# A gated recurrence on one core: another order for the products of half B, and for three VectorE operations

## The chip, the core and the metric

The kernel runs on one core of one Trainium2 chip. The metric is device time in microseconds for one execution. Times of one kernel are given as the median of several executions; the profile is of one execution, taken by the hardware profiler.

## What is computed

A recurrent layer over 512 steps with a batch of 8 and 512 units, plus a residual. Cut to what matters:

```python
def step(h, x_t):
    fused = sigmoid(concatenate([x_t, h], -1) @ w_W + w_b)
    r, z = split(fused, 2, axis=-1)          # hidden_state, output_state
    memory = x_t @ wx_W + wx_b + r * (h @ wh_W + wh_b)
    h_new = z * h + (1 - z) * tanh(memory)
    return h_new, h_new
_, hs = scan(step, h0, xT)                   # 512 steps
return x + swapaxes(hs, 0, 1)
```

Everything is in float32. What is written below as hh is `h @ wh_W + wh_b`. A step needs the whole h of the step before, so the steps follow one another strictly.

## The kernel before

**How the work is tiled.** The 512 units lie as four blocks of 128: block k holds, on 128 partitions, the units with which product k is made. Half A is the two blocks 0 and 1, half B the blocks 2 and 3. The state of each half lies transposed in SBUF (hTA and hTB), so that it can be the stationary operand of a matmul; a ring of eight buffers for each half holds the states of eight steps, four steps side by side in one buffer ("slots", GS = 4). A product `A2`, say, is one block k = 2 of the state against the weight columns of bank A, as four matmuls, one for each group of 32 columns of the array (line 136 issues all of them). In the trace every such matmul stands as two passes, so that one product is 8 records.

**What goes where.** There are three PSUM banks for the products of a step, each in two copies that alternate every four steps (`WH`, line 25): bank A (192 columns) takes hh, z and r of half A; bank Z (64 columns) takes z of half B; bank B (128 columns) takes r and hh of half B. Each bank has to have its products with all four blocks before it can be read. Blocks 0 and 1 need hTA of the step before, blocks 2 and 3 need hTB.

**TensorE's order** is written out by hand, in line 23, and run in lines 212 to 217 for each step: the names of bank and block in turn, and at the end one of four parts of the input product for a later group of four steps (`xp`, 384 columns, `prefill`). With the order before, the first three products need hTA alone (A0, B0, A1), then A2 and A3 (hTB), so that bank A is complete after five products; then the rest of B; then the four of Z.

**The elementwise part of a step** is in the functions of lines 229 to 290, and the order in which they are called (lines 292 to 303) is the order of VectorE's queue; the schedule is set by hand (`manual_schedule`), so nothing is moved. For half hf (0 is A, 1 is B):

- `turn_r`: VectorE transposes the r columns out of PSUM (tr, line 231), then ScalarE's sigmoid writes md0 (line 150).
- `turn_h`: VectorE transposes hh out of PSUM into md1 (md in the trace, line 243).
- `turn_z`: VectorE transposes z (tz, line 231), then ScalarE makes z (zA or zB) and 1 - z (hd0).
- `memory`: VectorE forms r * hh + x part with one scan instruction (m, line 263), then ScalarE's tanh writes hd1.
- `kept`: VectorE multiplies z and the old state (line 274), also into hd1; it waits for ScalarE's z.
- `update`: VectorE forms the new state with a second scan (hTA or hTB, line 283); it waits for tanh and for `kept`.

After these follow one transpose of the input part (line 179), on some steps a ScalarE copy that seeds the next banks (lines 157 and 174), and GpSimd's residual addition (line 314). SP issues the loads of x and the stores of the output, one of each in 16 steps.

The core of the order before is:

```python
        turn_r(0)
        turn_h(0)
        turn_z(0)
        memory(0)
        turn_h(1)
        kept(0)
        turn_r(1)
        update(0)
        turn_z(1)
        memory(1)
        kept(1)
        update(1)
```

Of the kernel before, what the change touches and what calls it, by code (L numbers as in the profile page):

```python
# [19 lines left out]
DVE_FILL = 5  # L20
SYNC = mybir.DependencyInfo(mybir.DependencyClass.Sync, mybir.DependencyReason.DATA)

ORDER = "A0 B0 A1 A2 A3 B1 B2 B3 Z0 Z1 Z2 Z3"

WH = {"A": slice(0, 192), "Z": slice(192, 256), "B": slice(256, 384)}

# [4 lines left out]
def tile_cond_rnn_residual(  # L31
# [44 lines left out]
    def load_x(c):  # L76
        if c < NCH:
            t_ = xin_p.tile([P, NQ, TC * B], F32, tag="xin", name=f"xin_{c}")
            nc.sync.dma_start(out=t_, in_=x[c].rearrange("p (k n) -> p k n", k=NQ))  # L79
            xins[c] = t_  # L80
# [36 lines left out]
    def state(hf, i):  # L117

        s = i % GS
        return hT[hf][i % NH][:, B * s : B * s + B, :, 1]  # L120
# [14 lines left out]
    def mm(out_, lhsT, rhs, start=False):  # L135
        nc.tensor.matmul(  # L136
            out_, lhsT, rhs, start=start, stop=False, skip_group_check=True
        )
# [10 lines left out]
    def act(key, *args, **kw):  # L149
        inst = nc.scalar.activation(*args, **kw).ins  # L150
        if key in written:
            tc.declare_no_dep(inst, written[key], reason="ordered through VectorE")
        written[key] = inst

    def seed(g):

        nc.scalar.copy(xps[g % 2], bias)

    def prefill(g):

        c, t0 = divmod(g * GS, TC)
        for k in range(NQ):
            for j in range(NQ):
                mm(
                    xps[g % 2][32 * j : 32 * j + 32, 64:448],
                    xins[c][:, k, t0 * B : t0 * B + 32],
                    wx[:, k, j, :],
                )
            yield

    def spread(g, names):

        for n in names:
            nc.scalar.copy(banks[g % 2][n], xps[g % 2][:, XP[n]])

    def turn_x(g, e):

        c0 = XP["X"].start + 32 * e
        nc.vector.transpose(
            md1[g % 2][:, e // 2, :, e % 2, 1], xps[g % 2][:, c0 : c0 + 32]  # L180
        )

    def take(it, n=None):
        while n is None or n > 0:
            if next(it, it) is it:
                return
            n = None if n is None else n - 1
# [14 lines left out]
    for i in range(T):  # L202
        g, s = divmod(i, GS)
        c, t = divmod(i, TC)
        ps = banks[g % 2]
        if t == 0:
            load_x(c + 3)
            ot = out_p.tile([P, NQ, TC, B], F32, tag="ot", name=f"ot_{c}")
        if s == 0:
            pre = prefill(g + 2) if g + 2 < NG else iter(())  # L210

        for n in ORDER.split():
            bank, k = n[0], int(n[1])
            hs = hT[k // 2][i % NH][:, :, k % 2, 1]
            for j in range(NQ):
                mm(ps[bank][32 * j : 32 * j + 32, :], hs, wh[:, k, j, WH[bank]])
        take(pre, 1)

        rows = slice(B * s, B * s + B)
        def flat(t_):  # L220
            return t_.rearrange("p n c s -> p (n c s)")

        raw = {
            "h": (ps["A"][:, :HU], ps["B"][:, HU:]),
            "z": (ps["A"][:, HU : 2 * HU], ps["Z"]),
            "r": (ps["A"][:, 2 * HU :], ps["B"][:, :HU]),
        }

        def turned(n, hf):
            t_ = work.tile([P, 2, 32], F32, tag=f"t{n}{hf}", name=f"t{n}{hf}_{i}")  # L230
            nc.vector.transpose(t_.rearrange("p c n -> p (c n)"), raw[n][hf])  # L231
            return t_[:, :, rows]

        def turn_r(hf):
            act(
                ("r", hf, g % 2, s),
                md0[hf][g % 2][:, rows, :, 1].rearrange("p n c -> p c n"),
                turned("r", hf),
                AF.Sigmoid,
            )  # L240

        def turn_h(hf):
            inst = nc.vector.transpose(  # L243
                md1[g % 2][:, hf, :, :, 0].rearrange("p n c -> p c n"), raw["h"][hf]
            ).ins

            if hf == 0 and i + 1 - NH in pool_done:
                tc.add_manual_dep(inst, pool_done[i + 1 - NH].name, SYNC)

        def turn_z(hf):  # L250
            tz = turned("z", hf)
            act(("z", hf, i % 2), zs[hf][i % 2], tz, AF.Sigmoid)
            act(
                ("zc", hf, i % 2),
                hd0[hf][i % 2][:, :, :, 1].rearrange("p n c -> p c n"),
                tz,
                AF.Sigmoid,
                scale=-1.0,
            )

        def memory(hf):
            m = work.tile([P, B, 2, 2], F32, tag=f"m{hf}", name=f"m{hf}_{i}")
            nc.vector.tensor_tensor_scan(  # L263
                flat(m),
                flat(md0[hf][g % 2][:, rows]),
                flat(md1[g % 2][:, hf, rows]),
                0.0,
                ALU.mult,
                ALU.add,
            )  # L270
            act(("n", hf, i % 2), hd1[hf][i % 2][:, :, :, 0], m[:, :, :, 1], AF.Tanh)

        def kept(hf):
            nc.vector.tensor_tensor(
                hd1[hf][i % 2][:, :, :, 1],
                zs[hf][i % 2].rearrange("p c n -> p n c"),
                state(hf, i),
                ALU.mult,
            )

        def update(hf):
            s1 = (i + 1) % GS
            nc.vector.tensor_tensor_scan(  # L283
                flat(hT[hf][(i + 1) % NH][:, B * s1 : B * s1 + B]),
                flat(hd0[hf][i % 2]),
                flat(hd1[hf][i % 2]),
                0.0,
                ALU.mult,
                ALU.add,
            )  # L290

        turn_r(0)
        turn_h(0)
        turn_z(0)
        memory(0)
        turn_h(1)
        kept(0)
        turn_r(1)
        update(0)
        turn_z(1)  # L300
# [4 lines that stand above are left out]
        if g + 1 < NG:  # L305
            turn_x(g + 1, s)
            if s == 0:
                spread(g + 1, "A")
            elif s == 1:
                spread(g + 1, "BZ")  # L310
            elif s == 3 and g + 3 < NG:
                seed(g + 3)
        for hf in range(2):
            pool_done[i + 1] = nc.gpsimd.tensor_tensor(  # L314
                ot[:, 2 * hf : 2 * hf + 2, t, :].rearrange("p c n -> p n c"),
                xins[c][:, 2 * hf : 2 * hf + 2, t * B : t * B + B].rearrange("p c n -> p n c"),
                state(hf, i + 1),
                ALU.add,
            ).ins
        if t == TC - 1:  # L320
            nc.sync.dma_start(out=out[c], in_=ot.rearrange("p k t b -> p (k t b)"))
            xins.pop(c)
# [62 lines left out]
```

## Time and profile before

| what | value |
|---|---|
| median of 3 executions | 1726.7 us (1726.22 to 1728.58) |
| the profiled execution's own time | 1726.31 us |
| span of the profiled execution | 1724.5 us |
| TensorE matmuls busy | 1706.2 us, 99% of the span |
| TensorE weight loads busy | 1489.8 us, 86% |
| VectorE busy | 1138.6 us, 66% |
| ScalarE busy | 894.8 us, 52% |
| GpSimd busy | 252.9 us, 15% |
| granted TensorE clock | 0.997 |

How to read it: a name such as `A<-wh,hTA` is the output and the inputs of an instruction. PE is TensorE's matmuls, PEld its weight loads, DVE is VectorE, ACT ScalarE, POOL GpSimd. The busy time of matmuls counts overlapping records once and their ends are modelled, so that 99% doesn't say by itself that TensorE works at its full rate; the distances between starts say more. A wait is put down to the instruction that came last. Times inside a step are given from the start of the first matmul of A0, in ns, where they are medians over the steps of the trace.

### The profile page before, as it was taken

The page shows a single profiled execution, that of the slowest core. Times are in us where ns is not written, and L with a number is a line of the kernel's source. Part 1 is how long each engine was busy: PE and PEld are TensorE (multiplying, and loading weights), DVE is VectorE, ACT ScalarE, POOL GpSimd, SP SyncE. Part 2 cuts the span into 40 slices and gives each one's busy share as a digit, 9 for nine tenths or more (in the row PEclk, how much of TensorE's full clock was granted, in tenths as well). Part 3 has the DMA queues.
Part 4 walks back from the last instruction along what each step waited for, and adds up shares of the span by engine and source line. Part 5 has one row for each costly group of instructions (what it writes and reads, how often), then busy time and mean ns, then how long its engine had stood idle before and what let it go on. Part 6 is the DMA issues. An engine that isn't in the chain of part 4 may idle for free.

```text
span 1724.5 us, 121032 instructions
## 1 busy us (share of the span) xinstructions
PE 1706.2 (99%) x53312; PEld 1489.8 (86%) x53312; DVE 1138.6 (66%) x6663; ACT 894.8 (52%) x4610; POOL 252.9 (15%) x1048
## 2 busy tenths in 40 slices
PE   7999999999999999999999999999999999999998
PEld 5888888888888888888888888888888888888887
DVE  2666666666666666666666666666666666666666
ACT  3555555555555555555555555555555555555554
POOL 1111111111111111111111111111111111111111
PEclk9999999999999999999999999999999999999999
DMA  4000000000000000000000000000000000000000
GB/s 179 17 4 17 17 17 17 10 11 17 17 17 16 5 17 17 17 16 5 17 17 17 17 17 5 17 17 17 17 4 17 16 17 16 5 17 11 11 11 10
DMA packets 11232, 31.09 MB, mean 18 GB/s; under 512 B 1360, under 2 KB 1360, under 8 KB 10704
## 3 DMA queue, kind: packets, MB, share of 16 engines
q1 hardware_dynamic: 10704, 23.35, 3.9%
q8 instruction: 416, 6.82, 1.6%
q14 instruction: 112, 0.92, 0.2%
HBM read 14.96 MB, written 8.39 MB: 14 GB/s over the span
## 4 chain that ended last, share of the span: by engine, by line
PE 98%; DMA 1%; DVE 0%; issue 0%; SPq 0%; ACT 0%; POOLq 0%; POOL 0%; DVEq 0%
PE A L136 39%; PE B L136 25%; PE xp L136 19%; PE Z L136 14%; DMA hin<-in_h_dram 1%; DMA wx<-in_wx_dram 0%; DVE tr L231 0%; ACT md0A L150 0%; DVE hTA L283 0%; DVE m L263 0%; SPq L85 0%; DVE md L243 0%; SPq L79 0%; POOLq L379 0%; POOL ot L314 0%
## 5 line engine op out<-in xcount | busy, mean ns | idle before, releaser
L136 PE MATMUL A<-wh,hTA 128*32 128x192 f32 x8192 | 555.6, 327 | 9.5 <-DVE hTB L125 7.3
L136 PEld LDWEIGHTS A<-wh,hTA 128*32 128x32 f32 x8192 | 321.3, 137 | 184.6 <-DVE hTA L283 176.2
L136 PE MATMUL B<-wh,hTA 128*32 128x128 f32 x8192 | 450.9, 273 | 0.0
L136 PE MATMUL A<-wh,hTB 128*32 128x192 f32 x8192 | 448.3, 327 | 0.0
L136 PE MATMUL xp<-wx,xin 128*32 128x384 f32 x4096 | 444.2, 486 | 0.0
L231 DVE STREAM_TRANSPOSE tr<-A 128x64 f32<-128x64 f32 x512 | 128.0, 250 | 470.0 <-PE A L136 470.0
L150 ACT ACTIVATE md0A<-tr 128x16 f32<-128x16 f32 x512 | 121.1, 236 | 487.9 <-DVE tr L231 487.9
L136 PEld LDWEIGHTS B<-wh,hTA 128*32 128x32 f32 x8192 | 364.7, 136 | 1.6
L136 PE MATMUL B<-wh,hTB 128*32 128x128 f32 x8192 | 336.4, 273 | 0.0
L136 PEld LDWEIGHTS A<-wh,hTB 128*32 128x32 f32 x8192 | 302.4, 137 | 33.0 <-DVE hTB L283 1.2
L314 POOL TENSOR_TENSOR ot<-xin,hTA 128x16 f32<-128x16 f32 x512 | 125.5, 245 | 1119.5 <-DVE hTA L283 1031.6
L136 PEld LDWEIGHTS B<-wh,hTB 128*32 128x32 f32 x8192 | 266.6, 137 | 0.0
L136 PE MATMUL Z<-wh,hTB 128*32 128x64 f32 x8192 | 240.6, 226 | 0.0
L136 PE MATMUL Z<-wh,hTA 128*32 128x64 f32 x8192 | 235.0, 223 | 0.0
L136 PEld LDWEIGHTS Z<-wh,hTA 128*32 128x32 f32 x8192 | 218.5, 141 | 0.0
L136 PEld LDWEIGHTS Z<-wh,hTB 128*32 128x32 f32 x8192 | 200.1, 148 | 0.0
L314 POOL TENSOR_TENSOR ot<-xin,hTB 128x16 f32<-128x16 f32 x512 | 124.5, 243 | 348.5 <-DVE hTB L283 343.2
L150 ACT ACTIVATE md0B<-tr 128x16 f32<-128x16 f32 x512 | 119.2, 233 | 70.8 <-DVE tr L231 0.7
L283 DVE TENSOR_TENSOR_SCAN hTB<-hd0B,hd1B 128x32 f32<-128x32 f32 x512 | 115.2, 225 | 52.7
L263 DVE TENSOR_TENSOR_SCAN m<-md0B,md 128x32 f32<-128x32 f32 x512 | 147.6, 288 | 0.0
L243 DVE STREAM_TRANSPOSE md<-B 128x64 f32<-128x64 f32 x512 | 146.9, 287 | 0.0
L243 DVE STREAM_TRANSPOSE md<-A 128x64 f32<-128x64 f32 x512 | 139.0, 271 | 0.0
(43 smaller groups left out, 1835.8 us busy)
## 6 DMA issues: line engine op xcount, KB each, us to landing
xin<-in_x_dram SPq DMA_DIRECT2D x32, 256.0 KB, 2.9
out_dram<-ot SPq DMA_DIRECT2D x32, 256.0 KB, 2.1
wx<-in_wx_dram SPq DMA_DIRECT2D x4, 768.0 KB, 6.7
wh<-in_wh_dram SPq DMA_DIRECT2D x4, 768.0 KB, 13.5
bias<-in_bias_dram SPq DMA_DIRECT2D x4, 64.0 KB, 2.0
hin<-in_h_dram SPq DMA_DIRECT2D x1, 16.0 KB, 14.8
```

The source lines that it names most:

```text
L136: nc.tensor.matmul(out_, lhsT, rhs, start=start, stop=False, skip_group_check=True)
L150: inst = nc.scalar.activation(*args, **kw).ins
L231: nc.vector.transpose(t_.rearrange("p c n -> p (c n)"), raw[n][hf])
L243: inst = nc.vector.transpose(md1[g % 2][:, hf, :, :, 0].rearrange("p n c -> p c n"), raw["h"][hf]).ins
L263: nc.vector.tensor_tensor_scan(flat(m), flat(md0[hf][g % 2][:, rows]), flat(md1[g % 2][:, hf, rows]), 0.0, ALU.mult, ALU.add,)
L283: nc.vector.tensor_tensor_scan(flat(hT[hf][(i + 1) % NH][:, B * s1 : B * s1 + B]), flat(hd0[hf][i % 2]), flat(hd1[hf][i % 2]), 0.0, ALU.mu ...
L314: pool_done[i + 1] = nc.gpsimd.tensor_tensor(ot[:, 2 * hf : 2 * hf + 2, t, :].rearrange("p c n -> p n c"), xins[c][:, 2 * hf : 2 * hf + 2, ...
```

## The change

Two lines of order are changed, and nothing else:

```diff
-ORDER = "A0 B0 A1 A2 A3 B1 B2 B3 Z0 Z1 Z2 Z3"
+ORDER = "A0 B0 A1 A2 A3 B1 Z0 B2 Z1 B3 Z2 Z3"
...
         turn_h(0)
         turn_z(0)
         memory(0)
+        kept(0)
         turn_h(1)
-        kept(0)
         turn_r(1)
         update(0)
         turn_z(1)
```

On TensorE the products Z0 and Z1, which need hTA alone, move in between the products of bank B, so that B3 is followed by Z2 and Z3. On VectorE `kept` of half A (z * h) moves from behind the transpose of hh of half B to in front of it; behind it now stand the transposes of hh and r of half B, and then the update of half A. The instructions are the same in number and shape, and the queues of ScalarE, GpSimd and SP hold the same order.

## The prediction

> **What bounds the kernel now.** I read the page first for the chain that ended last, then that chain in order of time over one step, then who waits for whom, then VectorE's own timeline over the same step. The chain lies on TensorE almost wholly:
>
> ```profile
> PE 98%; DMA 1%; DVE 0%; issue 0%; SPq 0%; ACT 0%; POOLq 0%; POOL 0%; DVEq 0%
> ```
>
> The chain in order of time, one step of the recurrence (columns: start, length, what):
>
> ```profile
> 1004.10 0.33 PE A L136 x8
> 1004.43 0.22 PE B L136 x8
> 1004.65 0.97 PE A L136 x24
> 1005.62 0.64 PE B L136 x24
> 1006.26 0.48 PE Z L136 x29
> 1006.74 0.67 PE xp L136 x8
> 1007.41 0.25 PE A L136 x5
> ```
>
> A step lasts 1007.41 - 1004.10 = 3.31 us without a hole. Times 512 steps that is 1695 of the span's 1724.5; the rest is the lead-in and the tail. Each product of the code stands here as two passes over four column groups, 8 records. A product into A costs 0.97/3 = 0.32, into B 0.64/3 = 0.21, into Z 0.48/4 = 0.12, and the input product xp 0.67. By columns (192, 128, 64, 384) that is 1.7 ns each, but Z takes 1.9: the narrow products alone do not stream at the others' rate. Within the Z run, the starts of successive passes in this trace are 55, 57, 57, 63, 61, 63, 62 and 63 ns apart: the first two or three after a wide product go at 55 to 57[...].
>
> The waits say what is nearly as long as TensorE's own work:
>
> ```profile
> PEld A L136 <- DVE hTA L283: 176.2, 506, 0.5
> ...
> PEld A L136 <- DVE hTB L283: 1.2, 7, 0.2
> ```
>
> The weight load of A0 waits for hTA in nearly every step, behind the cover of xp. The load of A2 waits for hTB too, but its wait is hidden behind A1's stream. VectorE over the same step (start, length, operation):
>
> ```profile
> 1002.35 0.25 DVE L231 STREAM_TRANSPOSE tr<-A 128x64 f32<-128x64 f32 x1 [0.92 <-PE A L136]
> 1002.52 0.27 DVE L243 STREAM_TRANSPOSE md<-A 128x64 f32<-128x64 f32 x1
> 1002.65 0.21 DVE L231 STREAM_TRANSPOSE tz<-A 128x64 f32<-128x64 f32 x1
> 1002.90 0.23 DVE L263 TENSOR_TENSOR_SCAN m<-md0A,md 128x32 f32<-128x32 f32 x1
> 1003.04 0.28 DVE L243 STREAM_TRANSPOSE md<-B 128x64 f32<-128x64 f32 x1
> 1003.19 0.15 DVE L274 TENSOR_TENSOR hd1A<-zA,hTA 128x16 f32<-128x16 f32 x1
> 1003.24 0.23 DVE L231 STREAM_TRANSPOSE tr<-B 128x64 f32<-128x64 f32 x1
> 1003.45 0.22 DVE L283 TENSOR_TENSOR_SCAN hTA<-hd0A,hd1A 128x32 f32<-128x32 f32 x1
> 1003.60 0.22 DVE L231 STREAM_TRANSPOSE tz<-Z 128x64 f32<-128x64 f32 x1
> 1003.78 0.29 DVE L263 TENSOR_TENSOR_SCAN m<-md0B,md 128x32 f32<-128x32 f32 x1
> 1004.10 0.18 DVE L274 TENSOR_TENSOR hd1B<-zB,hTB 128x16 f32<-128x16 f32 x1
> 1004.38 0.23 DVE L283 TENSOR_TENSOR_SCAN hTB<-hd0B,hd1B 128x32 f32<-128x32 f32 x1
> ```
>
> What to see: hTB starts at 1004.38; the weight-load timeline has the first load off it at 1004.66 (0.28 later), and A2's matmul at 1004.74. Over the middle 490 steps the load of A2 comes a median 70 ns ahead of its matmul, that of A0 130 ns ahead. What lead is the least? In steps 1 to 7, where hTB is late (load 28.61, matmul 28.64), 31 ns stand there, but the pass after it starts some 26 ns late, so about 55 is needed. So the slack is 15 ns for hTB and 75 for hTA: TensorE is the bound, and the ring hTB, A2, A3, VectorE, hTB is only just shorter.
>
> [...] the trace shows no product out of the code's order. [...] Z passes start 57 to 63 ns after their loads, whose records last 133 to 164. [...] start-to-start spacings, not durations, price VectorE's queue. The trace agrees: md<-A lasts 0.27 and tz starts 0.13 after it. [...]
>
> **The change, part by part.** No instruction is added or removed; ScalarE, GpSimd and SP keep their order, DMAs too.
>
> *TensorE order.* Before, three B products follow A3; after, B1 Z0 B2 Z1 B3, then Z2 Z3. Two Z products of two passes each stand in front of B3: 55 + 57, and on to the next B some 59, so 116 ns each, 232 together (bounds 220 and 250). B is complete 232 ns later; Z is complete at about the same time, because the products behind it are the same two. The gain: Z0 and Z1 use only the quick first passes, so of 491 ns for Z now about 473 stay, 18 ns a step less (bounds 0 and 57, the latter if all eight ran at 54).
>
> *VectorE: kept(0) in front.* The product z*h of half A (0.15) now waits for ScalarE's zA, which ends a median 2552 ns after A0's start; with the 32 ns that md0B to m shows, it starts at 2584 instead of 2633. In front of it nothing changes. Behind it now stand hh and r of B, and the update of A. Before, the update came 267 ns after kept(0), and that wait, not tanh, set it (tanh ended 76 ns ahead, where 32 are enough elsewhere). That wait goes. What is late next is B itself.
>
> *hh of B.* Before, B's last matmul starts at 2119 after A0; a wide A needs 380 from its last matmul start to the transpose, B 54 less by its shorter stream, so 326: B is ready at 2445, and the transpose at 2485 was set by VectorE's queue (142 behind m). After: 2119 + 232 + 326 = 2677, and kept(0) has long started (2584). [...] I take 2685 between the two, so hh of B is 200 ns late, and VectorE idles in front of it for the first time.
>
> *r of B, then the update of A.* hh to r with nothing between: 131, as md<-A to tz. r to the update: 148 as hh to kept(0), or 174 as tr to md; I take 160. The update comes 291 after hh, at 2976, against 2900 before: hTA is 76 ns late. Its slack was 75, so A0 is just met.
>
> *hTB.* From the update of A to that of B is 928 (925 to 933 in nine steps of ten): tz<-Z, zB, kept(1), update, all unchanged, and Z is ready in time (last Z matmul start 2654, plus 380 less 100 for its narrower stream = 2934; tz due at 2976 + 142 = 3118). A second path, r of B, md0B, m, tanh, update, comes to 131 + 239 + 34 + 232 + 32 + 245 + 34 + 220 + 32 = 1199 after hh; the first to 291 + 928 = 1219. So the first decides, and half B is late as half A is: 76 ns, against 15 of slack.
>
> *The ring, as a sum.* From A2's load to the transpose of A, in the steps where that load is late: 975. From there to hh of B: B's last matmul comes 708 after A's now, 940 after the change, less 54: 886. Then 291 + 928 + 279 (update to load). Sum 975 + 886 + 291 + 928 + 279 = 3359, against a mean of 3312 in the middle steps now. TensorE's own sum would be 3307 - 18 = 3289, so it waits about 70 ns a step, in front of A2. 3359 - 3312 = 47 ns, times 512 = 24 us. The profiled execution took 1726.31 (span 1724.5), 0.4 under the median of 1726.7; so 1751.
>
> **Rivals.** (1) TensorE stays the bound and the Z passes saved come through: 18 x 512 = 9 us, 1717. For it: the chain is 98% TensorE, and a wait of the update goes. It needs the ring below 3305, that is 54 ns less than my sum. Its loose terms: Z passes at 54 (12 less), hh to update at 262 (29 less), A2's load to transpose at the smallest seen, 954 (21 less): all three must fall together. Chance 0.10. (2) Nothing measurable (within 0.2%, 3.5 us, which is about what this measurement can tell): the ring at 3305 to 3319. It takes half of those reductions. Chance 0.09. (3) Much slower: the update behind r of B takes as long as before behind r (210), and hh is held by kept(0) (2708): 3359 + 50 + 23 = 3432, 120 ns a step, 61 us, 1788. For it: the pair r, update is 210 apart in every step now; against it: that gap ends with kept(0)'s result, which is early after the change. Chance 0.06. The forecast itself, ring at 3320 to 3415: 0.75.
>
> **How the numbers follow.** The forecast's own range is 1731 to 1779: 3320 and 3415 against 3312. The range to hold 8 in 10 takes in most of (2) and the beginning of (3): 1726 to 1785, leaving out (1), a little of (2) and part of (3). Faster 0.10, same 0.09, slower 0.81.
>
> **What would show it.** VectorE must show an idle stretch in front of md<-B, released by PE B, in every step, about 40 to 100 ns after kept(0) has begun; hTA and hTB in front of the A loads; holes of TensorE in front of A<-hTB, not of A<-hTA; a step of about 3.36; the update of A 0.26 to 0.31 after md<-B. If hTA's load is the late one, or Z still ends the step without a hole, the sum is wrong. What would make it wrong most easily is the spacing of hh, r and update on VectorE with all their inputs ready, which no step of the trace shows, and the 232 ns of the moved products.

## The result, and the profile after

The changed kernel takes 1737.28 us (median of 6, 1735.98 to 1739.07) against 1726.98 us before: ratio 1.0059, 95% interval 1.0049 to 1.007. It is slower by 10.3 us. The forecast was slower by 24 us, 1751, with a range of 1726 to 1785. The span of its profiled execution is 1735.1 us.

The chain that ended last, in order of time, one step of the changed kernel (start, length, what):

```profile
1004.30 0.33 PE A L136 x8
1004.63 0.22 PE B L136 x8
1004.85 1.00 PE A L136 x24
1005.85 0.22 PE B L136 x8
1006.07 0.11 PE Z L136 x8
1006.18 0.22 PE B L136 x8
1006.40 0.11 PE Z L136 x8
1006.52 0.23 PE B L136 x8
1006.75 0.24 PE Z L136 x16
1006.98 0.65 PE xp L136 x8
1007.63 0.33 PE A L136 x8
```

The step is 1007.63 - 1004.30 = 3.33 us, where it was 3.31. The chain still names TensorE alone, and yet TensorE is no longer what sets the time. Two entries grew: A1 to A3, 1.00 against 0.97, and the three B products together, 0.67 against 0.64. Z and xp shrank by 0.02 each (Z is 0.11 + 0.11 + 0.24 = 0.46 now), which makes up for B, so the longer A is what counts. Why A grew is seen where the first matmul of A2 starts right behind its weight load. In the changed kernel:

```profile
1004.96 0.38 PEld L136 LDWEIGHTS A<-wh,hTB 128*32 128x32 f32 x12
...
1004.99 0.54 PE L136 MATMUL A<-wh,hTB 128*32 128x192 f32 x8
```

In the kernel before:

```profile
1004.66 0.62 PEld L136 LDWEIGHTS A<-wh,hTB 128*32 128x32 f32 x16
...
1004.74 0.88 PE L136 MATMUL A<-wh,hTB 128*32 128x192 f32 x16
```

Before, 0.08 lay between the two; now 0.03 does, and over the middle 490 steps a median 26 ns against 71. The pass after it starts 192 ns later instead of 163. So TensorE waits some 29 ns in each step for hTB, hidden inside a matmul's record.

VectorE's timeline over the step before:

```profile
1002.59 0.25 DVE L231 STREAM_TRANSPOSE tr<-A 128x64 f32<-128x64 f32 x1 [0.88 <-PE A L136]
1002.76 0.27 DVE L243 STREAM_TRANSPOSE md<-A 128x64 f32<-128x64 f32 x1
1002.90 0.21 DVE L231 STREAM_TRANSPOSE tz<-A 128x64 f32<-128x64 f32 x1
1003.14 0.22 DVE L263 TENSOR_TENSOR_SCAN m<-md0A,md 128x32 f32<-128x32 f32 x1
1003.39 0.18 DVE L274 TENSOR_TENSOR hd1A<-zA,hTA 128x16 f32<-128x16 f32 x1
1003.48 0.30 DVE L243 STREAM_TRANSPOSE md<-B 128x64 f32<-128x64 f32 x1
1003.66 0.21 DVE L231 STREAM_TRANSPOSE tr<-B 128x64 f32<-128x64 f32 x1
1003.79 0.18 DVE L283 TENSOR_TENSOR_SCAN hTA<-hd0A,hd1A 128x32 f32<-128x32 f32 x1
1003.89 0.22 DVE L231 STREAM_TRANSPOSE tz<-Z 128x64 f32<-128x64 f32 x1
1004.17 0.23 DVE L263 TENSOR_TENSOR_SCAN m<-md0B,md 128x32 f32<-128x32 f32 x1
1004.39 0.18 DVE L274 TENSOR_TENSOR hd1B<-zB,hTB 128x16 f32<-128x16 f32 x1
1004.68 0.23 DVE L283 TENSOR_TENSOR_SCAN hTB<-hd0B,hd1B 128x32 f32<-128x32 f32 x1
```

hh of B (md<-B) starts 0.89 after tr<-A, where it started 0.69 after it. But the update of A follows it after 0.31 instead of 0.41, lasts 0.18 instead of 0.22, and tz<-Z comes 0.10 behind it instead of 0.15. So of the 0.20 that hh is late, hTB is late by less than a third (2.09 after tr<-A, against 2.03). There is almost no idle time of VectorE in front of hh (0.2 us in the whole trace, in one step): z*h with its 0.18 stands over it. The wait shows elsewhere, among the waits:

```profile
ACT md0B L150 <- DVE tr L231: 140.1, 501, 0.6
```

(total in us, times, longest); before, these were 0.7 us in 3 times.

The ring that goes through hTB (load of A2, tr<-A, hh of B, update of A, update of B, and the load of A2 in the next step), as means over the middle 490 steps (ns):

| piece of the ring | sum in the prediction | kernel before | changed kernel |
|---|---|---|---|
| load of A2 to tr<-A | 975 | 995 | 959 |
| tr<-A to hh of B | 886 | 696 | 895 |
| hh of B to update of A | 291 | 414 | 305 |
| update of A to update of B | 928 | 928 | 894 |
| update of B to load of A2 | 279 | 279 | 278 |
| sum, which is the step | 3359 | 3312 | 3331 |

The distances between starts around a closed ring add up to the step in any kernel, so the sum by itself doesn't say what sets the step. That the ring does is seen from its first piece: 995 before, it is down to 959, next to the least that any step here shows, 954. It is seen more plainly in the last seven steps, which have no input product, so that TensorE has some 0.65 us less to do in each. Two loads of A2 in a row there, first in the kernel before, then in the changed one:

```profile
1711.35 0.54 PEld L136 LDWEIGHTS A<-wh,hTB 128*32 128x32 f32 x16 [0.17 <-DVE hTB L283]
1714.62 0.54 PEld L136 LDWEIGHTS A<-wh,hTB 128*32 128x32 f32 x16 [0.17 <-DVE hTB L283]
...
1721.82 0.54 PEld L136 LDWEIGHTS A<-wh,hTB 128*32 128x32 f32 x16 [0.17 <-DVE hTB L283]
1725.15 0.54 PEld L136 LDWEIGHTS A<-wh,hTB 128*32 128x32 f32 x16 [0.17 <-DVE hTB L283]
```

Both wait openly for hTB. The kernel before now needs 3.27 us a step (a median 3269 ns), 43 less than in its middle steps. The changed kernel needs 3.33 (3323), almost what it needs in its middle steps: taking work from TensorE hardly helps it.

3331 - 3312 = 19 ns, times 512 = 9.7 us, which is the loss but for 0.6 us.

### The profile page after: what moved, and what is told of

Read it like the earlier page. It is cut to its first block, busy times and chain, and to the rows that moved or that the text cites. A ratio compares the mean times of both kernels' runs of the same rounds, so it can differ in the third digit from the quotient of the medians.

```text
span 1735.1 us, 121032 instructions
## 1 busy us (share of the span) xinstructions
PE 1716.4 (99%) x53312; PEld 1410.7 (81%) x53312; DVE 1139.7 (66%) x6663; ACT 911.2 (53%) x4610; POOL 253.1 (15%) x1048
## 4 chain that ended last, share of the span: by engine, by line
PE 98%; DMA 1%; DVE 1%; issue 0%; SPq 0%; ACT 0%; POOLq 0%; POOL 0%; DVEq 0%
PE A L136 40%; PE B L136 26%; PE xp L136 19%; PE Z L136 14%; DMA hin<-in_h_dram 1%; DMA wx<-in_wx_dram 0%; DVE tr L231 0%; ACT md0A L150 0%; SPq L85 0%; DVE m L263 0%; DVE hd1A L274 0%; DVE hTA L283 0%; DVE md L243 0%; SPq L79 0%; POOLq L379 0%
## 5 line engine op out<-in xcount | busy, mean ns | idle before, releaser
L136 PE MATMUL A<-wh,hTA 128*32 128x192 f32 x8192 | 527.7, 327 | 9.9 <-DVE hTB L125 7.3
L136 PEld LDWEIGHTS A<-wh,hTA 128*32 128x32 f32 x8192 | 269.3, 137 | 221.3 <-DVE hTA L283 212.7
L136 PE MATMUL B<-wh,hTA 128*32 128x128 f32 x8192 | 416.8, 273 | 0.0
L136 PE MATMUL B<-wh,hTB 128*32 128x128 f32 x8192 | 383.8, 276 | 0.0
L136 PEld LDWEIGHTS A<-wh,hTB 128*32 128x32 f32 x8192 | 273.7, 142 | 76.6 <-DVE hTB L283 12.3
L136 PEld LDWEIGHTS B<-wh,hTA 128*32 128x32 f32 x8192 | 326.3, 136 | 10.8
L136 PE MATMUL Z<-wh,hTA 128*32 128x64 f32 x8192 | 305.9, 220 | 0.0
L136 PEld LDWEIGHTS Z<-wh,hTA 128*32 128x32 f32 x8192 | 273.5, 136 | 0.0
L136 PEld LDWEIGHTS B<-wh,hTB 128*32 128x32 f32 x8192 | 232.3, 145 | 0.0
L263 DVE TENSOR_TENSOR_SCAN m<-md0B,md 128x32 f32<-128x32 f32 x512 | 116.1, 227 | 29.4 <-ACT md0B L150 0.2
```

What stands on the lines that cost most here:

```text
L136: nc.tensor.matmul(out_, lhsT, rhs, start=start, stop=False, skip_group_check=True)
L263: nc.vector.tensor_tensor_scan(flat(m), flat(md0[hf][g % 2][:, rows]), flat(md1[g % 2][:, hf, rows]), 0.0, ALU.mult, ALU.add,)
```

## The experiments

The comparisons below are each with runs of the kernel before on the same chip (1726.04 us for the first three, 1726.02 for the other four).

**One part of the change alone.** TensorE's new order with VectorE's old one:

```diff
-ORDER = "A0 B0 A1 A2 A3 B1 B2 B3 Z0 Z1 Z2 Z3"
+ORDER = "A0 B0 A1 A2 A3 B1 Z0 B2 Z1 B3 Z2 Z3"
```

> TensorE's new order alone; kept(0) stays behind hh of B. Theory 1 (the ring hTB - A2 - A3 - B3 - hh - r - update - hTB, lengthened by the two Z products in front of B3): hh is as late as in the changed kernel (about 895 ns after tr of A), but the update of A follows kept(0), which now follows hh: 148 + 267 = 415 ns after hh against 305, and an update that waits costs some 35 ns more behind it. Ring 3331 + 110 + 35 = 3476 ns, so about 1790 to 1815 us. Theory 2 (kept(0), which waits for ScalarE's zA in front of hh, is what made the changed kernel slower): without it no loss from that, so 1727 or less. Theory 3 (TensorE itself is slower when B and Z alternate): about 1737, as the changed kernel.

1819.2 us, ratio 1.054 (1.0525 to 1.0554); mean step 3490 ns. That is 4 us above theory 1's span and far from the other two theories' times. VectorE's timeline shows theory 1's order of events:

```profile
1001.79 0.30 DVE L243 STREAM_TRANSPOSE md<-B 128x64 f32<-128x64 f32 x1
1001.97 0.14 DVE L274 TENSOR_TENSOR hd1A<-zA,hTA 128x16 f32<-128x16 f32 x1
1002.02 0.24 DVE L231 STREAM_TRANSPOSE tr<-B 128x64 f32<-128x64 f32 x1
1002.22 0.23 DVE L283 TENSOR_TENSOR_SCAN hTA<-hd0A,hd1A 128x32 f32<-128x32 f32 x1
1002.36 0.22 DVE L231 STREAM_TRANSPOSE tz<-Z 128x64 f32<-128x64 f32 x1
```

hh to the update of A is 0.43 (mean 433, 18 more than the 415 expected: z*h comes 173 after an hh that has waited, not 148) and tz follows the update after 0.14, as before the change. The pieces of the ring are 956 + 895 + 433 + 929 + 278 = 3491. So late B by itself costs 93 us in this place; moving z*h away from behind hh takes most of that back.

**The other part alone.** VectorE's new order with TensorE's old one:

```diff
+        kept(0)
         turn_h(1)
-        kept(0)
         turn_r(1)
```

> VectorE's new order alone; TensorE's order as before. Theory 1 (late B is the cost): B is there early, the update of A comes a little earlier or at the same time and no longer waits; TensorE is the bound at 3307 ns a step, mean 3305 to 3312, so 1723 to 1728 us. Theory 2 (kept(0) waiting for zA in front of hh is the cost: hh starts some 99 ns behind kept(0) in the changed kernel, whatever B does): hh at 890 ns after tr of A as in the changed kernel, about 1735 to 1738. Theory 3 (TensorE's alternation): as before, 1727.

1731.64 us, ratio 1.0034 (1.0022 to 1.0046); mean step 3320. Theory 1 as I had put it falls here: B is early, and the kernel is slower all the same. Of theory 2 the place of hh comes true (890), its time of 1735 to 1738 doesn't.

```profile
1002.88 0.18 DVE L274 TENSOR_TENSOR hd1A<-zA,hTA 128x16 f32<-128x16 f32 x1
1002.98 0.30 DVE L243 STREAM_TRANSPOSE md<-B 128x64 f32<-128x64 f32 x1
1003.14 0.21 DVE L231 STREAM_TRANSPOSE tr<-B 128x64 f32<-128x64 f32 x1
1003.27 0.18 DVE L283 TENSOR_TENSOR_SCAN hTA<-hd0A,hd1A 128x32 f32<-128x32 f32 x1
```

hh starts a mean 94 ns behind z*h, and 889 after tr<-A, although B's last matmul began 572 ns ahead of it, where 339 are enough in the changed kernel. What holds it is z*h, which waits for ScalarE's zA (it starts 32 ns after zA's end in every step). The pieces of the ring are 961 + 889 + 298 + 894 + 279 = 3321. So in the changed kernel two things set hh at nearly the same moment: z*h at 889, B at 895.

**One Z product in front of B3 instead of two**, with VectorE's new order:

```diff
-ORDER = "A0 B0 A1 A2 A3 B1 Z0 B2 Z1 B3 Z2 Z3"
+ORDER = "A0 B0 A1 A2 A3 B1 Z0 B2 B3 Z1 Z2 Z3"
```

> Both orders new, but one Z product only in front of B3 (B1 Z0 B2 B3 Z1 Z2 Z3). Theory 1: B is complete about 117 ns earlier than in the changed kernel, so hh waits for kept(0) and not for B; the ring falls by 0 to 45 ns to 3285 to 3331, TensorE's own sum is about 3302 ns; mean step 3303 to 3325, so 1722 to 1733 us, nearer to 1723 if kept(0) to hh can be as short as 55 ns. Theory 2: 1737 as the changed kernel. Theory 3: half of the changed kernel's loss, about 1732.

1730.2 us, ratio 1.0025 (1.0016 to 1.0035); mean step 3320, the same as with no Z product moved, and hh 94 ns behind z*h and 889 after tr<-A as there. The time lies in theory 1's span, and as it said, hh waits for z*h and no longer for B. Only its hope for the lower end fails, since z*h to hh takes 94 and not 55. B is 119 ns later here than with the old order at no cost, because z*h holds hh anyway.

**What TensorE's order is worth by itself.** Both orders with the state of the step before the last as the stationary operand, so that the ring is open and TensorE's own time shows. These two runs compute something else, with the same instructions.

```diff
-            hs = hT[k // 2][i % NH][:, :, k % 2, 1]
+            hs = hT[k // 2][(i - 1) % NH][:, :, k % 2, 1]
```

> The changed kernel, but every product takes the state of the step before the last (another computation, same instructions and shapes), so TensorE no longer waits for the state and its own time per step shows. Theory 1 (the ring bounds the changed kernel, TensorE's own order is quicker than before): a step of about 3296 ns without holes, 1716 to 1721 us. Theory 3 (alternating B and Z makes TensorE slower): 3325 to 3331 ns, 1733 to 1738 us.

> The kernel before, changed in the same way (state of the step before the last). TensorE bounds it already by the trace, so about 3306 ns a step, 1722 to 1727 us; against the run with the new order this gives what the new order of products is worth on TensorE alone: about 10 ns a step, 5 us, by theory 1; a negative number by theory 3.

New order 1715.08 us (ratio 0.9934, 0.9919 to 0.9949), mean step 3301; old order 1719.14 us (0.9957, 0.9942 to 0.9972), mean step 3308. So the new order does save TensorE 7 ns a step, some 4 us, and theory 3 falls. The 3301 also fits the changed kernel: its step of 3331 less the 29 in front of A2 is 3302. Both times lie below their expected spans, mainly because the last seven steps take some 2690 ns with the old order and 2830 with the new one, where the kernel before takes 3270. In the changed kernel's trace a part of why it isn't 18 shows too: the Z passes save some 22 ns (the first two of each pair come at 56 and 57), but the B pass behind each of the first two pairs goes at 115 instead of 109, which gives 12 back.

**Late B without the wait of z*h.** In the changed kernel, z*h of half A takes the z of the step before, so that its input is always there (another computation again):

```diff
-                zs[hf][i % 2].rearrange("p c n -> p n c"),
+                zs[hf][(i + 1) % 2 if hf == 0 and i > 0 else i % 2].rearrange("p c n -> p n c"),
```

> The changed kernel, but kept(0) takes the z of half A of the step before (another value, same operation), so that it no longer waits for ScalarE's zA. If late B alone is enough to set hh: hh stays at 885 to 895 ns after tr of A and the step at 3320 to 3331, 1732 to 1737 us. If kept(0)'s wait is what sets hh and B's lateness only comes level with it by chance below: hh moves forward and the time falls to 1727 or less.

1737.17 us, ratio 1.0061 (1.0046 to 1.0076): the changed kernel's time to 0.1 us, at the upper end of the span expected if late B alone is enough.

```profile
1003.53 0.23 DVE L263 TENSOR_TENSOR_SCAN m<-md0A,md 128x32 f32<-128x32 f32 x1
1003.67 0.15 DVE L274 TENSOR_TENSOR hd1A<-zA,hTA 128x16 f32<-128x16 f32 x1
1003.87 0.30 DVE L243 STREAM_TRANSPOSE md<-B 128x64 f32<-128x64 f32 x1
1004.04 0.21 DVE L231 STREAM_TRANSPOSE tr<-B 128x64 f32<-128x64 f32 x1
1004.17 0.18 DVE L283 TENSOR_TENSOR_SCAN hTA<-hd0A,hd1A 128x32 f32<-128x32 f32 x1
```

z*h now starts right behind m and 0.20 ahead of hh, and hh has not moved: 894 after tr<-A, 340 after B's last matmul. B alone is enough.

**Neither wait.** The same edit with TensorE's old order:

> VectorE's new order with TensorE's order as before, and kept(0) with the z of the step before, so that neither B is late nor kept(0) waits. If these two waits are the whole loss: hh at about 730 ns after tr of A, TensorE the bound again at 3307 ns, 1723 to 1727 us. If moving kept(0) costs something else (its place in the queue): as the run with VectorE's order alone, 1731.

1725.16 us, ratio 0.9992 (0.9983 to 1.0001): no loss is left, and TensorE sets the step again (mean 3310).

```profile
1003.44 0.15 DVE L274 TENSOR_TENSOR hd1A<-zA,hTA 128x16 f32<-128x16 f32 x1
1003.50 0.31 DVE L243 STREAM_TRANSPOSE md<-B 128x64 f32<-128x64 f32 x1
1003.67 0.21 DVE L231 STREAM_TRANSPOSE tr<-B 128x64 f32<-128x64 f32 x1
1003.80 0.23 DVE L283 TENSOR_TENSOR_SCAN hTA<-hd0A,hd1A 128x32 f32<-128x32 f32 x1
1003.95 0.22 DVE L231 STREAM_TRANSPOSE tz<-Z 128x64 f32<-128x64 f32 x1
```

hh is at 765 after tr<-A (68 behind z*h; I had expected 730), the update of A at 1067 (1110 in the kernel before). Here that update has to wait for tanh (in both kernels tanh of A ends some 0.48 after m's start, which would be 1003.77 here, an estimate; the update starts at 1003.80), and it shows the slow form again: 0.23 long, tz 0.15 behind it, 0.93 to the update of B. It is the same queue order as in the run above, where it waited for nothing and took 0.18.

The four combinations of the two waits also show in the last seven steps, where the ring alone sets the step. With VectorE's new order they take (median, ns): neither wait 3226, z*h alone 3312, late B alone 3326, both 3323. The kernel before, with z*h behind hh, has 3269 there.

No run with the reference's computation was faster than the kernel before. Of the orders run here, those with z*h in front of hh, and with its own z, have a ring of some 3312 ns even with B early, and that is above TensorE's own 3301 to 3308; with z*h behind hh, late B costs 93 us. Other orders of VectorE's queue, which might let B be late at no cost, were not run.

## Why the prediction was right and wrong

**Right: the direction and the mechanism.** The sum's idea was that Z0 and Z1 make B late, that hh of B waits, and that the ring through hTB, no longer TensorE, sets the step. The runs with z*h's wait removed show it: with late B the loss stays (1737.17), without it the loss is gone (1725.16). B's last matmul starts 949 - 708 = some 240 ns later behind A's (predicted 232). hh of B is 208 ns later after A0's start (predicted 200), and 199 later after tr<-A (191 in the sum). TensorE waits in front of A2 and not of A0. Two signs that were named did not show: VectorE has no idle stretch in front of hh, and the chain has no hole; both waits lie under the record of another instruction. And one thing is level with B: z*h holds hh at 889 by itself. The prediction weighed that at 2708 after A0's start, 124 behind z*h, an estimate and no measured spacing, and then took a value below it; in the run where z*h alone holds hh, the spacing is 94. On its own this wait costs 5.6 us.

**Wrong: the size, 10.3 us instead of 24.** The time lies in the lower part of the range, but well below the sum's. The step that failed is "*hTB.* From the update of A to that of B is 928 (925 to 933 in nine steps of ten)", "all unchanged". It is 894. The 928 belongs to an update of A that has to wait for its input. The changed kernel's update waits for nothing when its turn comes; it then lasts 182 ns instead of 225 and lets tz<-Z start after 103 instead of 142. The run with TensorE's order alone, where the update waits for z*h, has 929; the run with VectorE's order alone has 894; the run with neither wait, where the update waits for tanh, has 931. By the prediction's own words the wait of the update goes, but the sum gave that a price in front of the update only, not behind it. These 34 ns alone are more than the 28 by which the sum was too long.

With them, "so the first decides" fails too. That first path, through zB and z*h of B, would now come some 8 ns before the second, through r of B and tanh: an estimate from the update of B starting 281 behind z*h of B in the kernel before and 289 now. In 94 of 100 of the middle steps the update of B starts 31 to 34 ns after tanh's end, which is as soon as a VectorE instruction follows the ScalarE result that it reads in the traces of the two kernels (the least is 31). From hh of B the second path takes 305 + 894 = 1199, just what the prediction had added up for it, but that is luck: hh to r is 173 and not 131, r to the sigmoid 242 and not 273, the memory scan 227 and not 245.

**The other terms.** The load of A2 to tr<-A, taken from steps 1 to 7 as 975, is 959, so the ring had more room before the change than was said: 959 + 1110 + 928 + 279 = 3276 against a step of 3312 is 36 ns, not 15, and the last seven steps of the kernel before say 43. Two terms went the other way: hh to the update is 305, not 291 (r follows an hh that has waited for B after 173, not 131, and the update follows r after 131, not 160), and tr<-A to hh 895, not 886. In all, -16 + 9 + 14 - 34 - 1 = -28, from 3359 to 3331.

**TensorE's saving** was put at 18 ns a step and is 7; the first rival, which lived on it, would have given 4 us and not 9. The B passes behind the moved Z, 115 instead of 109, were not in the sum. The saving played no part in the changed kernel's time, since there the ring decides. Two smaller slips bear on nothing: the first pass of Z starts a median 107 ns after its load and only the later ones after 54 to 61, and for the second rival two thirds of the three reductions are needed, not half.

## What to carry to other kernels

Where an engine in the chain is full, look for the ring of dependencies that is only just shorter, and add it up piece by piece before saving time on the full engine: 4 us of TensorE's time were on offer here, and the change that was to win them lengthened a ring with some 40 ns to spare by more than that. Here the spacing measured behind an instruction that waited (142) was not its spacing once it no longer waited (103); when a change takes a wait away, price both ends of the instruction. And two waits in front of the same instruction cost about the larger of the two here, not their sum (5.6 and 11.1 us alone, 10.3 together), so one of them can't be found by taking away the other.

## What was not expected of the hardware

An update scan of the same shape, in the same place of VectorE's queue, takes 182 ns and lets the next transpose start after 103 and TensorE's weight load after 236 when its inputs are long there (changed kernel, half A: tanh ends 167 ns ahead of it); when it has to wait for an input (kernel before), the three are 225, 142 and 278, all counted from its recorded start. The same shows for z*h of half A: 178 ns when it has waited for zA (changed kernel); when its input is there, a median 154 in the kernel before and 0.14 to 0.15 us in the views of three runs (TensorE's order alone, and the two with the z of the step before). Whether the recorded start lies earlier or the work is longer, these traces don't tell; the spacing to what follows grows with it, and so does the one to the load. And the memory scan of half B is longer the earlier it starts behind GpSimd's addition: a mean 288 ns where it starts a median 22 after it (kernel before), 250 at 67 (the run with neither wait), 227 at 116 (changed kernel), against 225 for half A, which overlaps none. In the trace before, the scan's end follows GpSimd's start by 314 ns in the median step. No run takes the addition away, so that it is the cause is not shown by experiment.
